# Per-node update steps on GpSimd behind a mask, and count reads placed by the steps beside them, in a two-layer graph kernel

## Chip, cores and metric

The kernel runs on one core of a Trainium2 chip. The metric is the time of the device in microseconds, the median of several runs. The engines are TensorE (PE, with its weight loads PEld), VectorE (DVE, `V` in the code), ScalarE (ACT, `A`), GpSimd (POOL, `G`) and SyncE (SP).

## The reference

There are 3327 nodes with 64 features each and an adjacency matrix `adj` of zeros and ones. The kernel pads 3327 to 26 blocks of 128. Cut to what matters:

```python
# layer 0: hyperbolic attention between connected nodes
h = relu(layernorm(x))
adj_att = sigmoid(left[:, None] + right[None, :] + b) * adj     # left, right from logmap0(h) @ w_att
support = einsum('ij,ijd->id', adj_att, logmap(h_i, h_j, c))    # a sum over neighbours j
x = x + proj(expmap(h, support, c), c)                          # node by node
# layer 1: a weighted sum over the last 100 neighbours of a row
h = relu(layernorm(x)); support = h @ weight
rank = cumsum(adj != 0, axis=1); deg = rank[:, -1:]; k = min(deg, 100)
pos = rank - (deg - k)
w = (adj != 0) * where(pos > 0, 0.5 ** (k - pos), 0)
x = x + w @ support + bias
```

Layer 0 has a large part for each pair of nodes (i, j) and a small part for each node i. Layer 1 needs, for each pair, how many neighbours of i come after j (the "count").

## The kernel before

`fast` does the work; `general` is a fall-back that a run-time flag selects and that isn't used with these inputs. The destination nodes i are cut into four strips of 8, 8, 6 and 4 blocks (`STRIPS`), and for each strip the source blocks j are walked from 25 down to 0. A strip of 8 or 6 blocks takes one source block in a round, the last strip two, so that a round has at most 1024 columns: 26, 26, 26 and 13 rounds, n = 0 to 90, so that strip 1 begins at round 26, strip 2 at 52 and strip 3 at 78. The text calls the strips 0 to 3.

In a round the engines do this:

- DVE: `edges` (L621) writes the mask of the adjacency block, in bf16; `pair_one` (L666) multiplies the attention by the adjacency; `pair_two` (L671) multiplies the result with the pair function out of PSUM.
- ACT: `gelus` (L870, L871), two activations in place in PSUM; `sigmoids` (L661), the attention's tanh.
- PE: `count` (L632, L633) adds the mask to a running count in PSUM; `products` (L678, L679) prepares the pair function; `total` (L691) sums over j.
- One of ACT (L650) and DVE (L652, L654) carries out `read`: it copies the count of this source block out of PSUM into `behind_lo`, `behind_hi` or `weight_of`, as integers. The next `count` has to wait for it. `ON_ACT` gives, for each strip, the share of the reads that go to ACT: 1/2, 5/8, 3/4, 1/2. In the last strip a round has two reads.

When a strip has ended, its sums are turned (`strip_out`, `turn`, `per_node`), and the per-node part, `post`, runs as a generator beside the rounds of the next strip. It is cut into portions: each `yield` ends one, and its value is what the portion counts. `BIG` (4) is a wide step of DVE, over all features of the strip's nodes; `LATER` (99) ends the portions of this call; `ACT` (100) asks for an activation, which is issued later in a round by `asked_of_act`. `advance(PORTIONS[k])` takes portions worth 4 once a round in strips 1 and 2, and worth 8 twice a round in strip 3. Many small steps, on one value a node, go to GpSimd while `hidden` is true, that is for the nodes of strips 0, 1 and 2; `after(time)` then lets as many calls pass as `time` takes at the round times in `ROUND`. For the last strip's nodes the small steps run on DVE and only the powers on GpSimd.

The steps of `post` in order: a product and two reduces (L1077 to L1081); small steps; a tanh on ACT (L1101); small steps; four wide steps that update x (L1137 `w`, L1139 `u`, L1141 and L1143 the additions to `xs`); a reduce (L1146) and a centring (L1148); a square on ACT (L1151) and a reduce (L1153); small steps; the features of layer 1 (L1159, L1162 on ACT, L1164). The wide steps of a strip's nodes run in the rounds of the strip after it.

Layer 1 comes last. Its matmuls (L1328) run over the source blocks in an order that has those of strip 3 at the end; `decode` (L1311 on ACT, L1314 and L1315 on DVE) turns counts into weights, and the rest of the per-node part of strips 2 and 3 runs beside it. GpSimd adds the bias (L1333).

The order on PE, DVE and ACT is the order in which the program issues (`manual_schedule`); each engine works through its own queue, and semaphores hold an instruction until its inputs are there. The main loop issues a round as follows:

```python
        gelus(n)
        asked_of_act()
        ...
        pair_one(n)
        if two:
            read(m, js(m)[0])
        if EARLY <= m + 1 < R:
            edges(m + 1)
```

after which come `count(m)`, `sigmoids(n + 1)`, the other `read(m)`, `products(n + 1)`, `pair_two(n)` and `advance`, with m = n + 1. So behind a mask on DVE stand, at most, a read and then `pair_two`.

Of the kernel before, what the change touches and what calls it, by code (L numbers as in the profile page):

```python
# [13 lines left out]
BF16 = mybir.dt.bfloat16  # L14
# [8 lines left out]
P = 128  # L23
N = 3327
NB = 26
# [7 lines left out]
AHEAD, LOADS = 1, 4  # L33
EARLY = 3
SGB, ADB = 5, 5
ON_ACT = ((1, 2), (5, 8), (3, 4), (1, 2))


PORTIONS, LAST = (2, 4, 4, 8), 8
BIG, LATER, ACT = 4, 99, 100  # L40
ROUND = (3.5, 3.5, 2.8, 1.9)

LEAD = 4
# [404 lines left out]
def fast(ctx, tc, x, adj_t, r, w_att, b_att, weight, bias, out, flag):  # L448

    nc = tc.nc  # L450
    V, A, G, T = nc.vector, nc.scalar, nc.gpsimd, nc.tensor
# [73 lines left out]
    def wide(t, n):  # L525
        return t[:, :, None].to_broadcast([P, n, D])
# [15 lines left out]
    post_pool = ctx.enter_context(tc.tile_pool(name="post", bufs=1))  # L542
# [3 lines left out]
    def behind(j):  # L546
        if j in JD:
            return weight_of[:, j - JD.start]
        return behind_of["lo"][:, j] if j < JD.start else behind_hi[:, j - JD.stop]
# [16 lines left out]
    ad_of, mask_of, sg_of, pq_of = {}, {}, {}, {}  # L566
# [36 lines left out]
    def span(n):  # L603
        k, lo, hi = rounds[n]
        return (hi - lo) * strips[k].F

    def js(n):
        k, lo, hi = rounds[n]
        return range(hi - 1, lo - 1, -1)
# [8 lines left out]
    def edges(n):  # L618
        mask_of[n] = mask = work.tile([P, FMAX], BF16, name="mask", bufs=3)
        args = mask[:, : span(n)], ad_of[n][:, : span(n)]  # L620
        V.tensor_scalar(*args, 0.0, None, op0=ALU.not_equal)  # L621
# [14 lines left out]
    def by_parity(t):  # L636
        return t.rearrange("p (r k) -> p r k", r=2)

    def read(n, j, on_act=None):
        k, lo, hi = rounds[n]  # L640
        S = strips[k]
        kept = behind(j)[:, S.i0 : S.i0 + S.F]
        num, den = ON_ACT[k]
        i = NB - 1 - j
        of = S.pc[:, : S.F]
        if j in JD:
            kept = by_parity(weight_of[:, j - JD.start])[:, :, S.i0 // 2 : (S.i0 + S.F) // 2]
            of = of.rearrange("p (k r) -> p r k", r=2)
        if on_act or (on_act is None and i * num // den != (i + 1) * num // den):
            A.activation(kept, of, AF.Relu, scale=128.0 if j in JD else 1.0)  # L650
        elif j in JD:
            V.tensor_scalar(kept, of, 0.0, 128.0, op0=ALU.max, op1=ALU.mult)  # L652
        else:
            V.tensor_scalar(kept, S.pc[:, : S.F], 0.0, None, op0=ALU.max)  # L654

    def sigmoids(n):

        S = strips[rounds[n][0]]
        sg_of[n] = sg = work.tile([P, FMAX], F32, name="sg", bufs=SGB)
        for j in js(n):  # L660
            A.activation(part(n, sg, j), S.left[:, : S.F], AF.Tanh, bias=right[:, j : j + 1], scale=0.5)  # L661
# [48 lines left out]
    def small(name):  # L710
        return pre.tile([P, NB], F32, name=name)
# [8 lines left out]
    m, rs = (small(n) for n in ("m", "rs"))  # L720
    v2, y2, t2 = (pre.tile([P, 2, NB], F32, name=n) for n in ("v2", "y2", "t2"))
    v, y = v2[:, 0], y2[:, 0]
    for hs in node_halves:
        n = hs.stop - hs.start
# [166 lines left out]
    for j in js(0):  # L891
        read(0, j, True)
# [10 lines left out]
    for b in (24, 20, 16, 12, 8, 4, 0):  # L903
        n = min(4, NB - b)
# [59 lines left out]
    def range_steps():  # L964
        t1 = post_pool.tile([P, NB], F32, name="st1")
        V.tensor_mul(t1, nrm, node)
        V.tensor_reduce(st[:, 0:1], t1, AX.X, ALU.max)
        yield 2
        V.scalar_tensor_tensor(t1, x2, c_c, t1, op0=ALU.mult, op1=ALU.mult)
        V.tensor_reduce(st[:, 1:2], t1, AX.X, ALU.max)  # L970
        yield 2
        V.tensor_mul(t1, bal, node)
        V.tensor_reduce(st[:, 2:3], t1, AX.X, ALU.max)
        yield 2
        V.tensor_reduce(st[:, 3:4], t1, AX.X, ALU.min)
        V.tensor_scalar(st[:, 3:4], st[:, 3:4], -1.0, None, op0=ALU.mult)
# [21 lines left out]
    class Asked:  # L998


        def __init__(self, engine, to):
            self.engine, self.to = engine, to

        def __getattr__(self, name):
            return lambda *args, **kwargs: self.to.append((getattr(self.engine, name), args, kwargs))

    def post(agg, k):


# [3 lines left out]
        b0, nb = STRIPS[k]  # L1013
        bs = slice(b0, b0 + nb)
        hidden = k + 1 < len(STRIPS)
# [3 lines left out]
        def tile_of(name, *dims):  # L1019
            return pool.tile([P, *dims], F32, name=name if hidden else name + "_last")  # L1020

        def mul(y, a, b):
            W.tensor_mul(y, a, b)
# [32 lines left out]
        def after(time):  # L1056

            for do, args, kwargs in asked_of_w:
                do(*args, **kwargs)  # L1059
                if not hidden:  # L1060
                    yield from [LATER] * 2 if kwargs.get("op") == ALU.pow else [1]
            asked_of_w.clear()
            if hidden:
                yield from [LATER] * math.ceil(time / ROUND[k + 1])
# [4 lines left out]
        hs, v, xs = hw[:, bs, :D], agg[:, :, :D], x_sb[:, bs]  # L1069

        dots, of_sum, of_end = tile_of("dots", 3, nb), tile_of("of_sum", 2, nb), tile_of("of_end", 2, nb)
        d, e = tile_of("d", 2, nb), tile_of("e", 2, nb)
        t0, t1, k_, y2, rn, rt = (tile_of(n, nb) for n in ("t0", "t1", "k", "y2", "rn", "rt"))
        u, w = tile_of("u", nb, D), tile_of("w", nb, D)
# [21 lines left out]
        root(rn, t0)  # L1096
        mul(t0, t0, rn)
        mul(t0, t0, sk[:, bs])
        yield from after(8.5)
        yield ACT  # L1100
        A.activation(k_, t0, AF.Tanh)  # L1101
        yield 0
# [31 lines left out]
        mul(of_end, of_end, both(rn))  # L1134
        mul(of_end[:, 0], of_end[:, 0], ih[:, bs])
        yield from after(16)
        V.tensor_mul(w, hs, wide(of_end[:, 0], nb))  # L1137
        yield BIG
        V.tensor_mul(u, v, wide(of_end[:, 1], nb))  # L1139
        yield BIG  # L1140
        V.tensor_add(xs, xs, w)  # L1141
        yield BIG
        V.tensor_add(xs, xs, u)  # L1143
        yield BIG

        V.tensor_reduce(t0, xs, AX.X, ALU.add)  # L1146
        yield BIG
# [50 lines left out]

    class Stage:
        def __init__(self, portions):  # L1200
            self.portions, self.asked = portions, False

    def advance(portions):
        for stage in stages:
            while portions > 0 and not stage.asked:
                portion = next(stage.portions, LATER)
                stage.asked = portion == ACT
                if portion >= LATER:
                    break
                portions -= portion  # L1210

    def asked_of_act():
        for stage in stages:
            if stage.asked:
                next(stage.portions)
                stage.asked = False

    def finish():
        for stage in stages:
# [4 lines left out]
    stages, rest_of_ahead = [Stage(range_steps())], last_of_ahead()  # L1224
# [3 lines left out]
    for n in range(2, R):  # L1228
        k, lo, hi = rounds[n]
        m, w = n + AHEAD, span(n)  # L1230
        ended, turned = (n > i and rounds[n - i - 1][1] == 0 for i in (1, 2))
        if n + LOADS < R:
            if rounds[n + LOADS][2] == NB:
                strip_in(rounds[n + LOADS][0])
            load(n + LOADS)
        fresh = EARLY <= m < R
        two = fresh and len(js(m)) == 2
        if two:
            count(m, js(m)[0])
        apart = k + 1 == len(STRIPS)  # L1240
        if turned and not apart:
            pa = turn(k - 1)
        if n >= 4 and (apart or not turned):
            total(n - 2)
        gelus(n)
        asked_of_act()
        if turned and not apart:
            finish()
            stages.append(Stage(per_node(k - 1, pa)))
        pair_one(n)  # L1250
        if two:
            read(m, js(m)[0])
        if EARLY <= m + 1 < R:
            edges(m + 1)
        if n == 2:
            for j in js(2):
                read(2, j, True)
        if n < 4:
            products(n + 1)
        if fresh:  # L1260
            count(m, js(m)[-1])
        if n + 1 < R:
            sigmoids(n + 1)
        if fresh:
            read(m, js(m)[-1])
        if 4 <= n < R - 1:
            products(n + 1)
        if n == 2:
            total(1)
        if ended:  # L1270
            strip_out(k - 1)
        if hi - lo > 1:
            advance(PORTIONS[k])
        if turned and apart:
            pa = turn(k - 1)
        pair_two(n)
        if turned and apart:
            finish()
            stages.append(Stage(per_node(k - 1, pa)))
        if n < 4:  # L1280
            next(rest_of_ahead)
            continue
        advance(PORTIONS[k])
        if turned and not apart:
            total(n - 2)
        if n > R - 3:
            next(range_end)
# [11 lines left out]
    with tc.tile_pool(name="l1", bufs=2, reuse_waits="tile") as l1, tc.manual_schedule(engines=IN_ORDER):  # L1299
# [35 lines left out]
        for i, j in enumerate(order):  # L1335
            for jn in every[: i + 1 + LEAD]:
                if jn not in weights:
                    weights[jn] = decode(jn)
            asked_of_act()
            advance(LAST)  # L1340
            for n in range(len(chunks)):
                add(j, weights[j], n)
            if i % 4 == 3 and i < STRIPS[-2][0]:
                bias(i - 3, 4)
# [93 lines left out]
```

## Time and profile before

| | us |
|---|---|
| median of 3 runs | 404.73 (404.49 to 406.21) |
| the profiled execution, whole | 406.06 |
| its span | 404.3 |
| busy in the span: PE, DVE, ACT, POOL | 353.7, 366.7, 355.8, 117.7 |

The span is what the profile covers, from the first to the last instruction. The profiled execution was 1.3 us longer than the median of the runs, so a change that is worked out from its rows is taken off its own time and then carried over to the median. On the timeline a row gives the start, the duration, the engine, the line, the operation, output and inputs, and shapes. Durations of one engine overlap by about 0.1 us, so that what an instruction costs its engine is better read from one start to the next. Round n is found by its L870 on ACT: round 31 starts at 145.45, round 32 at 149.35, round 40 at 178.07, round 50 at 214.15, round 54 at 227.97, round 57 at 237.26, round 76 at 292.65, round 90 at 346.71. The matmuls of layer 1 begin at 354.11.

### The profile page before, as it was taken

The page shows a single profiled execution, that of the slowest core. Times are in us where ns is not written, and L with a number is a line of the kernel's source. Part 1 is how long each engine was busy: PE and PEld are TensorE (multiplying, and loading weights), DVE is VectorE, ACT ScalarE, POOL GpSimd, SP SyncE. Part 2 cuts the span into 40 slices and gives each one's busy share as a digit, 9 for nine tenths or more (in the row PEclk, how much of TensorE's full clock was granted, in tenths as well). Part 3 has the DMA queues.
Part 4 walks back from the last instruction along what each step waited for, and adds up shares of the span by engine and source line. Part 5 has one row for each costly group of instructions (what it writes and reads, how often), then busy time and mean ns, then how long its engine had stood idle before and what let it go on. Part 6 is the DMA issues. An engine that isn't in the chain of part 4 may idle for free.

```text
span 404.3 us, 4738 instructions
## 1 busy us (share of the span) xinstructions
PE 353.7 (87%) x1460; PEld 150.3 (37%) x1460; DVE 366.7 (91%) x563; ACT 355.8 (88%) x407; POOL 117.7 (29%) x240
## 2 busy tenths in 40 slices
PE   0077899999999899999999899999979899899992
PEld 0053333333333333333333444444433333254462
DVE  3999899999999989999999999899999999899831
ACT  3589999999999899999999999999998999858710
POOL 8145200000000053870052052850240767241200
PEclk9999999999999899999999999999999999999997
DMA  7314545454547434543434435444563340000012
GB/s 208 142 42 133 170 144 154 131 159 148 160 146 229 152 107 156 156 155 107 153 115 149 149 119 156 133 139 120 158 191 106 114 148 0 0 2 1 2 39 54
DMA packets 23298, 48.99 MB, mean 121 GB/s; under 512 B 8789, under 2 KB 9245, under 8 KB 23265
## 3 DMA queue, kind: packets, MB, share of 16 engines
q1 hardware_dynamic: 20993, 47.66, 38.1%
q10 hardware_dynamic: 1808, 0.46, 0.6%
q0 software_dynamic: 464, 0.49, 0.5%
q8 instruction: 13, 0.21, 0.2%
q14 instruction: 20, 0.16, 0.1%
HBM read 46.40 MB, written 0.87 MB: 117 GB/s over the span
## 4 chain that ended last, share of the span: by engine, by line
DVE 39%; PE 24%; ACT 23%; issue 10%; DMA 1%; DVEq 0%; ACTq 0%
DVE sg L671 13%; DVE sg L666 11%; PE pw L1328 9%; ACT pq L870 7%; ACT sg L661 7%; PE po L691 6%; DVE behind_lo L654 3%; ACT pq L871 3%; ACT behind_lo L650 2%; PE pq L678 2%; PE pq L679 2%; DVE behind_hi L654 2%; DVE mask L621 2%; PE pc L632 2%; PE pw L1370 2%
## 5 line engine op out<-in xcount | busy, mean ns | idle before, releaser
L691 PE MATMUL po<-sg,hw 128*65 128x512 f32 (+1 forms) x364 | 160.2, 563 | 0.4 <-DVE st L987 0.4
L671 DVE SCALAR_TENSOR_TENSOR sg<-pq,sg 128x1024 f32<-128x1024 f32 (+1 forms) x91 | 103.7, 1140 | 4.3 <-ACT pq L871 3.8
L666 DVE SCALAR_TENSOR_TENSOR sg<-sg,ad 128x1024 f32<-128x1024 f32 (+1 forms) x91 | 104.2, 1146 | 0.2
L661 ACT ACTIVATE sg<-left_b,right 128x1024 f32<-128x1024 f32 (+2 forms) x103 | 99.5, 978 | 0.0
L871 ACT ACTIVATE pq<-pq 128x1024 f32<-128x1024 f32 (+1 forms) x91 | 86.2, 947 | 2.9
L870 ACT ACTIVATE pq<-pq 128x1024 f32<-128x1024 f32 (+1 forms) x91 | 87.1, 957 | 1.6 <-PE pq L679 1.3
L691 PEld LDWEIGHTS po<-sg,hw 128*65 128x65 f32 x364 | 49.2, 138 | 68.9 <-issue 54.2
L632 PE MATMUL pc<-mask,ca 128*128 128x512 bf16 (+1 forms) x175 | 63.5, 363 | 11.0 <-ACT behind_hi L650 3.2
L678 PE MATMUL pq<-iu,ju 71*128 71x512 f16 (+1 forms) x182 | 67.0, 368 | 1.7 <-ACT jz L807 0.8
L633 PE MATMUL pc<-mask,cb 128*128 128x512 bf16 (+1 forms) x182 | 64.9, 367 | 2.7 <-ACT behind_lo L650 1.7
L679 PE MATMUL pq<-iz,jz 128*128 128x512 f16 (+1 forms) x182 | 65.5, 367 | 0.0
L621 DVE TENSOR_SCALAR mask<-ad 128x1024 bf16<-128x1024 f32 (+1 forms) x91 | 58.8, 647 | 0.0
L1059 POOL TENSOR_TENSOR dots<-dots,ih 128x8 f32<-128x8 f32 (+1 forms) x3 | 3.7, 1223 | 131.0 <-DVE dots L1079 131.0
L633 PEld LDWEIGHTS <-cb 128*128 128x128 bf16 x182 | 17.7, 97 | 52.2 <-issue 40.5
L1328 PE MATMUL pw<-wt,s 128*128 128x512 bf16 (+1 forms) x154 | 31.4, 364 | 0.0
L632 PEld LDWEIGHTS <-ca 128*128 128x128 bf16 x175 | 17.1, 98 | 30.3 <-issue 18.0
L678 PEld LDWEIGHTS <-ju 71*128 71x128 f16 x182 | 17.9, 98 | 23.6 <-DVE sg L671 5.9
L679 PEld LDWEIGHTS <-jz 128*128 128x128 f16 x182 | 18.0, 99 | 18.9 <-issue 2.0
L650 ACT ACTIVATE behind_lo<-pc 128x1024 uint8<-128x1024 f32 (+2 forms) x29 | 24.9, 859 | 0.0
L1328 PEld LDWEIGHTS <-s 128*128 128x128 f16 x182 | 17.8, 99 | 18.2
L1333 POOL TENSOR_TENSOR x_sb<-x_sb,bias_b 128x256 f32<-128x256 f32 (+1 forms) x6 | 8.3, 1394 | 51.9 <-DVE w L1148 46.0
L650 ACT ACTIVATE behind_hi<-pc 128x1024 uint8<-128x1024 f32 (+2 forms) x25 | 21.8, 871 | 1.6 <-PE pc L633 1.5
(318 smaller groups left out, 347.3 us busy)
## 6 DMA issues: line engine op xcount, KB each, us to landing
ad<-in_adj_t SPq DMA_DIRECT2D x65, 512.0 KB, 3.5
ad<-in_adj_t SPq DMA_DIRECT2D x26, 384.0 KB, 3.1
out<-o SPq DMA_DIRECT2D x6, 128.0 KB, 1.9
left_b<-left_d SPq DMA_DIRECT2D x1, 512.0 KB, 4.3
x_sb<-in_x ACTq DMA_DIRECT2D x1, 416.0 KB, 5.5
x_sb<-in_x SPq DMA_DIRECT2D x1, 416.0 KB
left_b<-left_d SPq DMA_DIRECT2D x1, 384.0 KB
jz<-iz POOLq DMA_DIRECT2D x2, 128.0 KB, 2.6
```

What stands on the lines that cost most here:

```text
L621: V.tensor_scalar(*args, 0.0, None, op0=ALU.not_equal)
L632: T.matmul(S.pc[:, f0:f1], ca, S.before[:, f0:f1], start=False, stop=True, skip_group_check=True)
L633: T.matmul(S.pc[:, f0:f1], cb, now[:, f0:f1], start=S.first, stop=True, skip_group_check=True)
L661: A.activation(part(n, sg, j), S.left[:, : S.F], AF.Tanh, bias=right[:, j : j + 1], scale=0.5)
L666: V.scalar_tensor_tensor(sg, sg, 1.0, ad_of.pop(n)[:, :w], op0=ALU.add, op1=ALU.mult)
L671: V.scalar_tensor_tensor(sg, pq_of.pop(n)[:, :w], WD, sg, op0=ALU.add, op1=ALU.mult)
L678: T.matmul(part(n, pq, j, f0, f1), ju[:KB, j, :], S.iu[:, f0:f1], start=True, stop=False)
L679: T.matmul(part(n, pq, j, f0, f1), jz[:, j, :], S.iz[:, f0:f1], start=False, stop=True)
L691: T.matmul(po[: D + 1, : f1 - f0], hw[:, j, :], part(n, sg_of[n], j, f0, f1), start=j == NB - 1, stop=j == 0)
L870: A.activation(pq, pq, AF.Gelu, scale=-WG / QS)
L871: A.activation(pq, pq, AF.Gelu, scale=WH)
L1328: T.matmul(pw[n], s2[:, j].rearrange("p c d -> p (c d)"), w if r is None else w[:, r], start=j == order[0], stop=j == NB - 1)
```

## The change

The four wide update steps go from DVE to GpSimd for the nodes of strips 0, 1 and 2. Each is asked for with `yield POOL` and issued by a new `asked_of_pool`, straight after a mask was issued on DVE. Ahead of it GpSimd copies one column of that mask into `seen`, so that in GpSimd's queue the step comes after a wait for the mask. One step goes out in a round. Where no mask is issued in a round any more, or in layer 1, the step is issued without the copy. After the fourth step one call passes (`LATER`) before DVE goes on. The last strip's nodes keep their wide steps on DVE.

`ON_ACT` goes. In a strip with one read a round, a read goes to ACT if a portion that counted `BIG` was taken since the last read (`wide_step`); the other reads go to ACT and DVE in turn. In the last strip the lower of the two blocks is read on ACT and the other on DVE. The time that is let pass ahead of the tanh goes from 8.5 to 7.

```diff
-ON_ACT = ((1, 2), (5, 8), (3, 4), (1, 2))
-BIG, LATER, ACT = 4, 99, 100
+BIG, LATER, ACT, POOL = 4, 99, 100, 101
...
-        num, den = ON_ACT[k]
-        i = NB - 1 - j
+        if hi - lo > 1:
+            on_act = j == lo
...
-        if on_act or (on_act is None and i * num // den != (i + 1) * num // den):
+        if on_act is None:
+            on_act = wide_step[0] or not last_on_act[0]
+            if not wide_step[0]:
+                last_on_act[0] = on_act
+            wide_step[0] = False
+        if on_act:
             A.activation(kept, of, AF.Relu, scale=128.0 if j in JD else 1.0)
...
+    def tensor_mul(engine, *args):
+        engine.tensor_mul(*args)
+
+    def tensor_add(engine, *args):
+        engine.tensor_add(*args)
+
+    seen = post_pool.tile([P, 1], BF16, name="seen")
...
-        yield from after(8.5)
+        yield from after(7)
         yield ACT
...
         yield from after(16)
-        V.tensor_mul(w, hs, wide(of_end[:, 0], nb))
-        yield BIG
-        V.tensor_mul(u, v, wide(of_end[:, 1], nb))
-        yield BIG
-        V.tensor_add(xs, xs, w)
-        yield BIG
-        V.tensor_add(xs, xs, u)
-        yield BIG
+        for op, *args in ((tensor_mul, w, hs, wide(of_end[:, 0], nb)), (tensor_mul, u, v, wide(of_end[:, 1], nb)),
+                          (tensor_add, xs, xs, w), (tensor_add, xs, xs, u)):
+            if hidden:
+                yield POOL
+                op(G, *args)
+                yield 0
+            else:
+                op(V, *args)
+                yield BIG
+        if hidden:
+            yield LATER
...
                 portion = next(stage.portions, LATER)
-                stage.asked = portion == ACT
+                wide_step[0] |= portion == BIG
+                stage.asked = portion if portion in (ACT, POOL) else None
...
-    def asked_of_act():
+    def asked_of(engine):
         for stage in stages:
-            if stage.asked:
+            if stage.asked == engine:
                 next(stage.portions)
-                stage.asked = False
+                stage.asked = None
+
+    def asked_of_pool(n):
+        if any(stage.asked == POOL for stage in stages):
+            G.tensor_copy(seen, mask_of[n][:, :1])
+            asked_of(POOL)
...
         if EARLY <= m + 1 < R:
             edges(m + 1)
+            asked_of_pool(m + 1)
+        elif n > 4:
+            asked_of(POOL)
...
-            asked_of_act()
+            asked_of(ACT)
+            asked_of(POOL)
             advance(LAST)
```

More of the change, by code (lines that the diff above doesn't have):

```diff
@@ L654, in read @@
             V.tensor_scalar(kept, S.pc[:, : S.F], 0.0, None, op0=ALU.max)
+    wide_step, last_on_act = [False], [False]
     def sigmoids(n):
@@ L1200, in __init__ @@
         def __init__(self, portions):
-            self.portions, self.asked = portions, False
+            self.portions, self.asked = portions, None
     def advance(portions):
@@ L1338, in fast @@
                     weights[jn] = decode(jn)
-            asked_of_act()
+            asked_of(ACT)
+            asked_of(POOL)
             advance(LAST)
```

## The prediction

> **What bounds the kernel now.** I read the busy table first, the chain of waits second, then windows over the strips, then the timeline of three engines in a few rounds. The page alone doesn't decide:
>
> ```profile
> PE 353.7 (87%) x1460; PEld 150.3 (37%) x1460; DVE 366.7 (91%) x563; ACT 355.8 (88%) x407; POOL 117.7 (29%) x240
> DVE 39%; PE 24%; ACT 23%; issue 10%; DMA 1%; DVEq 0%; ACTq 0%
> ```
>
> The first line has DVE busiest, the second (the chain, by engine) has DVE in front. Both suggest that work taken off DVE pays in full. The windows say otherwise. The first row runs from ScalarE's start on round 32 to its start on round 54 (the bulk of strip 1 and the entry to strip 2), the second from round 57 to round 76 (strip 2). Columns: busy time of PE, weight loads, DVE, ACT, POOL.
>
> ```profile
> 149.35:227.97 78.62, 75.55 (x265) 28.58 (x263) 77.28 (x86) 77.92 (x86) 30.27 (x56) 1.00 0.46 144
> 237.26:292.65 55.39, 52.03 (x231) 24.89 (x230) 51.78 (x70) 54.79 (x74) 22.91 (x53) 1.00 0.48 142
> ```
>
> ACT is busy for 77.92 of 78.62 us and for 54.79 of 55.39: it has no idle time there. DVE has 1.3 and 3.6 us free. So in strips 1 and 2, where the edits lie, **ScalarE's own work sets the time, with DVE close behind**. The timeline of ScalarE in strip 1 gives its price list:
>
> ```profile
> 188.01 1.01 ACT L650 ACTIVATE behind_lo<-pc 128x1024 uint8<-128x1024 f32 x1
> 188.92 1.02 ACT L870 ACTIVATE pq<-pq 128x1024 f32<-128x1024 f32 x1
> 189.97 1.01 ACT L871 ACTIVATE pq<-pq 128x1024 f32<-128x1024 f32 x1
> 190.90 1.14 ACT L661 ACTIVATE sg<-left_b,right 128x1024 f32<-128x1024 f32 x1
> 191.94 1.01 ACT L870 ACTIVATE pq<-pq 128x1024 f32<-128x1024 f32 x1
> ```
>
> From start to start, two gelus and a tanh (L870, L871, L661) take 191.94 - 188.92 = 3.02 us a round, and a count read (L650) adds 0.91. The same timeline in strip 2 (768 wide) gives 2.37 and 0.70. DVE in strip 1, start to start: 1.14 (L666) + 0.60 (mask, L621) + 1.13 (L671) = 2.87 a round, 1.13 for a read (L654), 0.60 for a wide step. In strip 2: 2.20, 0.86, 0.60. PE: eight bf16 or f16 matmuls at 0.216 plus the 1.72 us sum of L691 = 3.45 a round in strip 1, three quarters of it (2.59) in strip 2.
>
> [...]
>
> ```profile
> 201.52 1.22 DVE L666 SCALAR_TENSOR_TENSOR sg<-sg,ad 128x1024 f32<-128x1024 f32 x1
> 202.65 0.69 DVE L621 TENSOR_SCALAR mask<-ad 128x1024 bf16<-128x1024 f32 x1
> 203.25 1.22 DVE L654 TENSOR_SCALAR behind_lo<-pc 128x1024 uint8<-128x1024 f32 x1
> 204.39 1.21 DVE L671 SCALAR_TENSOR_TENSOR sg<-pq,sg 128x1024 f32<-128x1024 f32 x1
> 201.68 2.92 POOL L1333 TENSOR_TENSOR x_sb<-x_sb,bias_b 128x256 f32<-128x256 f32 x2 [21.23 <-DVE w L1148]
> ```
>
> Two GpSimd additions of 256 elements take 2.92 us here; the shortest single one of L1333 in this trace takes 0.717. [...] In the other direction I see holds too: L666 at 30.44 takes 1.40 us and L919 at 33.02 takes 0.99 while L905 runs on GpSimd; elsewhere they take 1.22 and 0.68 to 0.69. [...] from the trace's shortest 256-element product (L905, 0.604) it is at most 1.21. I take 1.2, and 0.9 for 384.
>
> **The change, part by part.**
>
> *Wide steps to GpSimd.* Twelve DVE instructions go: eight of 0.60 and four of 0.47 (start to start), 6.7 us. In their place come twelve GpSimd products and sums at 1.2 or 0.9, and eight copies `seen` of one column, about 0.2 each (small copies of L1059 take 0.19). The four steps of strip 2's nodes find no later mask, so they have no `seen`; they run one behind the other after the small chain, which ends at 342.2 now, and are over by about 347. A released step starts about 0.3 us after the mask. [...] A 1.2 us step ends at 1.5. It delays the next L666 by 0.4 us where ScalarE reads, by nothing where DVE reads; in strip 2 by 0.6 or 0. The reads alternate in those four rounds, so the cost on DVE is 2 x 0.4 = 0.8 in strip 1 and 2 x 0.6 = 1.2 in strip 2. Bounds: 0, and a whole step (1.2) each. Behind the waiting `seen` on GpSimd's queue stands only its step; behind that, the reduce of L1146 on DVE, and a whole further round is put between them. A mask buffer is now also held by `seen`, but three buffers rotate.
>
> *Reads.* I followed the rule by hand. Strip 1: 6 reads are marked by a wide step and go to ScalarE, the other 20 alternate (10 there): 16, as before. Strip 2: 8 marked, 9 of 18 alternating: 17 instead of 19, and DVE reads 9 instead of 7. Strip 3: the lower block of a round reads on ScalarE, which is what 1/2 gave. Strip 0: alternating, as before.
>
> *ScalarE's sum.* Strip 2: two reads fewer, -1.4 us. Strip 1: equal count, moved. Rounds 25 to 30 have one read more, where ScalarE waits for PE (its starts there are 5.57 us apart); only about 0.5 of its 0.91 stays. Rounds 31 to 39 have 5 instead of 6: -0.9. Rounds 40 to 49 have 6 and 6. Net -0.4.
>
> *DVE's cover.* Rounds 40 to 49 cost DVE 28.7 + 4 reads 4.5 + 7 small steps 4.2 = 37.4 now, against ScalarE's 36.1; DVE falls 2.2 us behind and ScalarE doesn't stop, so the buffers carry that much. Afterwards: 37.4 - 2.4 + 0.8 = 35.8, under 36.1. In strip 2, rounds 68 to 75: 17.6 + 3 x 0.86 + 1.8 + 1.2 = 23.2 against ScalarE's 8 x 2.37 + 5 x 0.70 + 0.42 = 22.9, inside what the buffers carry. So the removed 4.8 us buy almost nothing by themselves: they only keep DVE from being late at the turn into strip 3 (rounds 77 to 82, where DVE sets the pace): -0.2.
>
> *Strip 3 and the end.* ScalarE sets 3.77 us a round there, unchanged. At the end L1137 to L1148 lie ahead of the last L671 on DVE; without them the last sums on PE may start up to 0.6 us earlier (PE's queue is full until then). GpSimd's steps collide with DVE there, so I take -0.3.
>
> *Layer 1.* The reduce and centring of strip 2's nodes move into it: +0.9 us of DVE. Last strip's features are written at 382.2 and PE first wants them near 385.2 (the first bank is read out at 386.07, four matmuls later), so 3 us cover it. Asking for the tanh earlier (7 for 8.5) costs nothing: in strips 1 and 2 it comes a round sooner, and GpSimd idles 6.4 and 8.3 us for it now; in strip 3 the round stays the same.
>
> Sum: -0.4 - 1.4 - 0.2 - 0.3 = **-2.3 us**. The profiled execution took 406.06 (span 404.3), so it would be 403.8; against the median of 404.73, 402.4.
>
> **Rivals.** (a) The sum above: 402.4, chance 0.50. (b) *DVE is the bound, as the chain has it.* Then 6.7 us less, two reads more (1.7): -5.0, 399.7. For it: 91% and 39%. Against: ScalarE's missing idle time. Chance 0.07. (c) *Nothing to be told from before*: ScalarE's 1.8 us are there, but GpSimd's holds give half back at the DVE-paced turn; 403.9, chance 0.28. This holds the case that the moved reads just trade idle time. (d) [...] a step begun after the mask runs into L666 and holds it in every one of the eight rounds of strips 1 and 2. DVE's slack is 1.1 us of strip 1 after the removal and a little under that in strip 2; with the 2.3 gained, 8 holds must exceed 4.3 us, 0.54 each, before the kernel is slower. Held for the whole 1.2 each: 9.6 - 4.3 = +5.3, 410.0; at 0.8 each, +2.1. [...] Chance 0.15.
>
> **Numbers.** About 0.5% (2.0 us) is what a measurement of this kernel can tell from no change. (a) lies 0.3 us beyond that line, and its terms are uncertain by 1.2 us in all, so some of it falls inside. Faster 0.52, same 0.34, slower 0.14. Range 400.4 to 406.0: down to near (b), up through (c) to the mild end of (d).
>
> **What would show it.** Right: ScalarE still without idle time in rounds 32 to 76, with 17 reads in strip 2; GpSimd's steps of 1.2 to 1.5 us that start after a mask; L666 late by about 0.4 us in every second of these rounds; layer 1 as long as before. Wrong: ScalarE waiting for `pq` or `sg` in rounds 40 to 45 or 68 to 72 [...], steps of over 2 us, or a longer gap ahead of the last strip's matmuls.

## The result, and the profile after

The changed kernel takes 405.36 us (median of 22 runs) where the kernel before took 405.87 beside it (22 runs): ratio 0.9998, interval 0.9987 to 1.001. Nothing that this measurement could tell apart has changed; the 0.5 us between the medians lies at the edge of that interval. The forecast was 402.4, 2.3 us faster than a median of 404.73. That median was of three runs; of 22 it is 405.87, so 1.1 us of the 3.0 between forecast and result come from the start of the sum and not from its terms.

In the page after, DVE is as busy as before, although twelve wide steps left it, and it still leads the chain of waits:

```profile
PE 354.5 (88%) x1460; PEld 151.0 (37%) x1460; DVE 367.1 (91%) x553; ACT 354.6 (88%) x405; POOL 135.7 (34%) x260
DVE 38%; ACT 28%; PE 18%; issue 12%; DMA 1%; DVEq 0%; ACTq 0%
```

DVE has ten instructions fewer (twelve steps went, two reads came) and is busy 0.4 us *longer* (366.7 before). So others of its instructions became longer. The windows of rounds 32 to 54 and 57 to 76 (same cuts as before, columns as before) place it: DVE is busy 2.9 us more in the second (54.72 for 51.78). There the four steps that left took 2.7 us; three reads more (eight instead of five) take 2.9, and the same 19 masks and 19 L672 take 2.3 more.

```profile
149.35:227.97 78.62, 75.17 (x266) 28.83 (x265) 77.27 (x83) 77.72 (x85) 34.57 (x60) 1.00 0.48 141
237.26:292.65 55.39, 53.46 (x237) 25.36 (x236) 54.72 (x70) 54.30 (x73) 31.37 (x58) 1.00 0.50 140
```

The timeline of GpSimd and of DVE in strip 1 of the changed kernel says why. L1014 and L1017 are the wide steps, L1238 is the copy into `seen`, L658 the count read on DVE, L672 is `pair_one`, L620 the mask:

```profile
177.24 1.04 POOL L1014 TENSOR_TENSOR u<-agg,of_end 128x512 f32<-128x512 f32 x1
178.24 2.02 POOL L1014 TENSOR_TENSOR w<-hw,of_end 128x512 f32<-128x512 f32 x1
180.34 1.59 POOL L1017 TENSOR_TENSOR x_sb<-x_sb,w 128x512 f32<-128x512 f32 x1
182.01 1.27 POOL L1017 TENSOR_TENSOR x_sb<-x_sb,u 128x512 f32<-128x512 f32 x1
183.23 1.19 POOL L1238 COPY seen<-mask 128x1 bf16<-128x1 bf16 x1
185.11 0.19 POOL L1238 COPY seen<-mask 128x1 bf16<-128x1 bf16 x1 [0.69 <-DVE mask L620]
```

```profile
177.56 1.80 DVE L672 SCALAR_TENSOR_TENSOR sg<-sg,ad 128x1024 f32<-128x1024 f32 x1
179.29 1.53 DVE L620 TENSOR_SCALAR mask<-ad 128x1024 bf16<-128x1024 f32 x1
180.74 1.21 DVE L658 TENSOR_SCALAR behind_lo<-pc 128x1024 uint8<-128x1024 f32 x1
```

**The gate is not there.** All four steps run in a row as soon as the small steps end, `u` even ahead of `w`, and the copies come after them. `IN_ORDER` holds PE, DVE and ACT, not GpSimd; its instructions were put in another order than the program's, and no step depends on `seen`. The unguarded steps hold DVE: L672 takes 1.80 instead of 1.21, the mask 1.53 instead of 0.68. Summed over the instructions after 140 us, such holds are 1.6 us in strip 1, 2.4 in strip 2 and 0.4 in strip 3.

**An account by stretches.** I cut the traces at ScalarE's starts of the first gelu of a round, at the start of layer 1's first matmul and at the end of its last. Two executions of the kernel before agree to 0.02 us in every stretch, so small differences can be read. The first column is the length before, the others are differences to it, in us:

```
rounds    before  changed  no_seen  no_wide  late_order  turn_reads  at_once  all_three
0-29      109.33   -0.02     0.00    +0.19     +0.49       +0.17      -0.04    +0.05
29-30       5.57   +0.01    -1.64    -1.64     -1.64       -1.64      -1.64    -0.09
30-40      36.03   -0.41    -0.40    -0.38     -0.40       -0.96      -0.40    -0.88
40-51      39.99   +0.37    +0.30    -0.01     -0.03       +1.78      +0.32    +0.03
51-55      13.76    0.00    -0.01    +0.01      0.00        0.00       0.00    +0.02
55-56       2.39   +1.36    +1.34    +1.34     +1.36        0.00      +1.35     0.00
56-68      34.79   -1.41    -1.41    -1.39     -1.42       -1.41      -1.42    -1.37
68-76      23.65   -0.02    -0.02    -0.70     -0.71        0.00      +0.01    -0.67
76-83      27.82   -0.29    -0.30    -0.30     -0.30       -0.29      -0.30    -0.29
83-90      26.24   -0.06    -0.06    -0.06     -0.06       -0.06      -0.06    -0.04
90-layer1   7.40   -0.61    -0.62    -0.61     -0.61       -0.60      -0.23    -0.24
layer 1    43.11   +0.65    +0.66    +0.81     +0.62       +0.64       0.00     0.00
sum       370.08   -0.43    -2.16    -2.74     -2.70       -2.37      -2.41    -3.48
```

(no_seen and the others are the experiments below; `at_once` is `strip3_at_once`.) The changed kernel gains 2.8 us in five stretches (30 to 40, 56 to 68, and the three from 76 to layer 1) and gives 2.4 back in three: rounds 40 to 51, 55 to 56 and layer 1. Rounds 68 to 76 should have gained 0.7 and didn't.

Two of the stretches go with TensorE's granted clock. In each of the fourteen profiles of this case 29 to 30 takes 5.5 to 5.6 us where a stretch of half clock begins in round 28, and 3.9 where none does; 55 to 56 takes 3.7 us in the ten profiles with one that begins in round 54, and 2.4 in the four without (the kernel before, twice, `turn_reads` and `all_three`). The windows 134.4 to 137.8 in the kernel before, and both places in the changed one and in `turn_reads` (the clock is the third number from the end):

```profile
134.40:137.80 3.40, 3.40 (x8) 1.15 (x7) 3.40 (x5) 3.37 (x5) 0.00 (x0) 0.58 0.46 140
```

```profile
134.40:137.80 3.40, 3.40 (x9) 1.21 (x7) 3.40 (x5) 3.37 (x5) 0.00 (x0) 0.64 0.51 140
230.00:233.40 3.40, 3.40 (x8) 1.19 (x7) 2.43 (x5) 3.37 (x6) 0.00 (x0) 0.64 0.46 130
```

```profile
134.40:137.80 3.40, 3.40 (x11) 1.17 (x9) 3.40 (x5) 3.37 (x5) 0.00 (x0) 1.00 0.47 137
230.00:233.40 3.40, 3.40 (x15) 1.57 (x14) 2.68 (x5) 3.37 (x6) 0.00 (x0) 1.00 0.51 163
```

Both places are turns from one strip to the next, where PE waits for the sums to be copied (1.83 us at the first in the changed kernel, 0.84 and 0.62 at the second). The changed kernel's two stretches of half clock are 3.41 us long (133.47 to 136.88 and 229.04 to 232.45, a granted clock of 0.50 in both). In the 3.41 us ahead of them PE was busy for 1.57 and 1.96 us, at a clock of 1.00. As much idle time isn't always followed by one: at the turn into strip 3 of the kernel before PE was busy for 1.67 of 3.41 us (294.00 to 297.41), and the clock is 1.00 there and in the 3.41 us after it. What sets off a stretch isn't shown. ScalarE's extra read of round 55 stands at the same turn, so that the 1.36 us there can't be put down to the read alone.

### The profile page after: what moved, and what is told of

Read it like the earlier page. It is cut to its first block, busy times and chain, and to the rows that moved or that the text cites. A ratio compares the mean times of both kernels' runs of the same rounds, so it can differ in the third digit from the quotient of the medians.

```text
span 404.6 us, 4764 instructions
## 1 busy us (share of the span) xinstructions
PE 354.5 (88%) x1460; PEld 151.0 (37%) x1460; DVE 367.1 (91%) x553; ACT 354.6 (88%) x405; POOL 135.7 (34%) x260
## 4 chain that ended last, share of the span: by engine, by line
DVE 38%; ACT 28%; PE 18%; issue 12%; DMA 1%; DVEq 0%; ACTq 0%
DVE sg L677 10%; DVE sg L672 9%; ACT sg L667 8%; ACT pq L876 8%; PE po L697 7%; ACT pq L877 4%; DVE behind_lo L658 3%; ACT behind_lo L654 2%; PE pq L684 2%; ACT behind_hi L654 2%; PE pq L685 2%; PE pc L631 2%; PE pc L632 2%; DVE mask L620 2%; PE pw L1397 2%
## 5 line engine op out<-in xcount | busy, mean ns | idle before, releaser
L677 DVE SCALAR_TENSOR_TENSOR sg<-pq,sg 128x1024 f32<-128x1024 f32 (+1 forms) x91 | 103.7, 1140 | 5.2 <-ACT pq L877 4.7
L672 DVE SCALAR_TENSOR_TENSOR sg<-sg,ad 128x1024 f32<-128x1024 f32 (+1 forms) x91 | 106.9, 1175 | 0.2
L620 DVE TENSOR_SCALAR mask<-ad 128x1024 bf16<-128x1024 f32 (+1 forms) x91 | 60.5, 666 | 0.0
L654 ACT ACTIVATE behind_lo<-pc 128x1024 uint8<-128x1024 f32 (+2 forms) x28 | 24.1, 860 | 0.0
L654 ACT ACTIVATE behind_hi<-pc 128x1024 uint8<-128x1024 f32 (+2 forms) x25 | 21.8, 871 | 2.2 <-PE pc L632 2.1
L658 DVE TENSOR_SCALAR behind_lo<-pc 128x1024 uint8<-128x1024 f32 (+2 forms) x20 | 20.1, 1003 | 0.1
```

What stands on the lines that cost most here:

```text
L672: V.scalar_tensor_tensor(sg, sg, 1.0, ad_of.pop(n)[:, :w], op0=ALU.add, op1=ALU.mult)
L677: V.scalar_tensor_tensor(sg, pq_of.pop(n)[:, :w], WD, sg, op0=ALU.add, op1=ALU.mult)
```

## The experiments

Theory A: ScalarE's work sets the pace, and what it gained was lost where the unguarded steps hold DVE, at the turn and in layer 1. Theory B: DVE had room for the holds. Rival: DVE sets the pace.

**The copies removed** (`no_seen`).

```diff
...
-            G.tensor_copy(seen, mask_of[n][:, :1])
```

> The changed kernel without the copies of the mask into seen; nothing else. Theory A: the copies gate nothing, so GpSimd's steps stay where they are and the starts of the rounds agree with those of the changed kernel to 0.1 us. If the copies did hold something back (a mask buffer, or the steps), rounds 40 to 46 or 68 to 74 would move by 0.3 us or more.

Ratio to before 0.9981 (0.9963 to 1.0). Apart from 29 to 30 the stretches agree with the changed kernel's within 0.07 us, and the holds on DVE are the same to 0.02 us (0.59, 0.85, 0.17 in strip 1). The copies gate nothing.

**The wide steps left out, and put back on DVE.** In `wide_on_dve` `op(G, *args)` is `op(V, *args)`; in `no_wide` the line is gone. Neither has `seen`.

> The changed kernel with the twelve wide steps of strips 0 to 2 left out, on GpSimd and DVE both (x of these nodes is not updated by layer 0). It is the most that taking these steps off DVE can bring. Theory A: no holds, so ScalarE's 0.4 and 0.7 us come back: 0.8 to 1.3 us ahead of the changed kernel, and not more, since ScalarE's own work is unchanged. Theory B: within 0.2 us of it. Rival (DVE sets the pace): 4 us ahead.

> The changed kernel with the twelve wide steps back on DVE, at the place where GpSimd's were asked for (behind a mask, one a round); reads and tanh as in the changed kernel. Theory A (ScalarE sets the pace, DVE close behind): DVE has 6.7 us more of its own and 4.4 us of holds less, so it stands about 2.3 us worse over three strips, most of it covered: 0 to 1 us after the changed kernel. Rival (DVE sets the pace, as the chain says): 2 us or more after it.

`no_wide`: ratio 0.9952 (0.9934 to 0.997), 1.8 us below before in the medians (403.74 against 405.56). Without any wide step rounds 40 to 51 are even with the kernel before and 68 to 76 gain 0.70: against the changed kernel that is 0.38 and 0.68. So the holds cost 1.06 us there, close to the 0.4 and 0.7 expected. The median is 1.5 us under that of `no_seen`, which ran beside it (403.74 for 405.24). The rival, with 4 us, falls.

`wide_on_dve`: ratio 1.0012 (0.999 to 1.0034). Rounds 40 to 51 take 0.57 more than before, 68 to 76 take 0.40 less, layer 1 takes 1.59 more since two of its wide steps moved into it. The median is 0.7 us over that of `no_seen` (405.90 for 405.24), within what was expected. Set against `no_wide`, which differs from it in the twelve steps alone, it is 2.2 us slower: 0.58 in rounds 40 to 51, 0.30 in 68 to 76, 0.27 in 76 to 83, 0.79 in layer 1 and 0.37 in the opening (rounds 0 to 29). So 6.7 us of DVE are worth about 2 us here: DVE is not the bound, but it isn't free either. In strip 2, work on DVE is cheaper than the unguarded steps on GpSimd (-0.40 against -0.02), in strip 1 dearer (+0.57 against +0.37).

**GpSimd kept in order** (`gpsimd_in_order`, whole main part; `late_order`, from round 20).

```diff
...
+        if n == 20:
+            ordered.close()
+            ordered.enter_context(tc.manual_schedule(engines=IN_ORDER | {mybir.EngineType.Pool}))
```

> The changed kernel with GpSimd's queue, too, kept in the order in which the main loop issues, so that each wide step really stands behind its copy of the mask. Theory A (the gate is missing in the changed kernel: the four steps ran in a row before any of the copies and held DVE's L672 and mask for 4.4 us): the steps start 0.2 to 0.4 us after a mask, DVE's stretched instructions add up to at most 2 us, ScalarE gets about 0.4 us back in strip 1 and 0.7 in strip 2, and the kernel ends 0.5 to 1 us before the changed one, near 404.3 where that has 405.0. Theory B (DVE had room for the holds, what was lost was lost on ScalarE at the turns): the steps move, the time does not (within 0.2 us).

> As the kernel with GpSimd's queue kept in order, but only from round 20 on, so that the opening of the kernel, which had become 4.1 us longer there, stays as in the changed kernel. Theory A: the opening is back to the changed kernel's; the wide steps stand behind their masks, ScalarE's loss of 0.37 us over rounds 40 to 51 and 0.68 us over rounds 68 to 76 are gone, and the kernel ends about 1 us ahead of the changed one, less if a stretch of half clock falls badly. Theory B: no difference (within 0.2 us).

The first is 0.59% slower (1.0059, 1.004 to 1.0079): GpSimd's products and loads of the opening were put in order too, and rounds 0 to 29 take 4.1 us more. It was expected ahead of the changed kernel and isn't; in rounds 40 to 51 and 68 to 76 it does what was expected (0.00 and -0.69). `late_order` keeps that and loses the opening's cost: ratio 0.9978 (0.9959 to 0.9997). Its GpSimd in strip 1:

```profile
178.24 0.19 POOL L1239 COPY seen<-mask 128x1 bf16<-128x1 bf16 x1 [2.16 <-DVE mask L620]
178.38 1.04 POOL L1015 TENSOR_TENSOR w<-hw,of_end 128x512 f32<-128x512 f32 x1
182.30 0.19 POOL L1239 COPY seen<-mask 128x1 bf16<-128x1 bf16 x1 [2.89 <-DVE mask L620]
182.44 1.04 POOL L1015 TENSOR_TENSOR u<-agg,of_end 128x512 f32<-128x512 f32 x1
185.30 0.19 POOL L1239 COPY seen<-mask 128x1 bf16<-128x1 bf16 x1 [1.82 <-DVE mask L620]
185.43 1.28 POOL L1018 TENSOR_TENSOR x_sb<-x_sb,w 128x512 f32<-128x512 f32 x1
```

and its DVE around the second step:

```profile
181.49 0.68 DVE L620 TENSOR_SCALAR mask<-ad 128x1024 bf16<-128x1024 f32 x1
182.09 1.21 DVE L677 SCALAR_TENSOR_TENSOR sg<-pq,sg 128x1024 f32<-128x1024 f32 x1
183.23 1.33 DVE L672 SCALAR_TENSOR_TENSOR sg<-sg,ad 128x1024 f32<-128x1024 f32 x1
```

A product takes 1.04 us, starts 0.3 us after the mask's end and overlaps L672 by 0.25; L672 is held for 0.12. Where DVE reads a count in between, it isn't held at all. The holds fall to 0.47 us in strip 1 and 1.02 in strip 2, and ScalarE doesn't feel them (-0.03 and -0.71, as without any wide step). Theory B falls, by these stretches: they are the same in `gpsimd_in_order`, `late_order` and `no_wide`. The medians alone would not show it, since the interval of `late_order` overlaps that of the changed kernel.

**The reads at the turns** (`turn_reads`).

```diff
+        if n in (31, 56):
+            on_act = False
```

> The changed kernel with two count reads given back to DVE: those issued in rounds 30 and 55, at the turns into strips 1 and 2, where the rule marks three reads in a row for ScalarE. Theory A (part of the loss is the reads that ScalarE takes at the turns): ScalarE's start of round 31 comes about 0.5 us earlier and that of round 56 by 0.7 to 1.4 us, kept up to round 76; DVE has 1.5 us or more to spare there. The kernel ends 1 us ahead of the changed one or a little more. If DVE has no room at the turns, the gain is gone by round 40 and round 60.

Ratio 0.9999 (0.9983 to 1.0016): the expected gain is not there. In the trace its parts came, 0.55 us more in rounds 30 to 40 and 1.36 in 55 to 56, but rounds 40 to 51 cost 1.78 instead of 0.37. The 1.36 is not the read's alone, for in this trace the clock is whole at that turn (1.00 at 230 to 233.4, above): two things changed at once. ScalarE arrives earlier, and the unguarded steps now meet other instructions of DVE. Two masks in a row are held, 1.53 and 1.76 for 0.68; the counts behind them come late, and ScalarE waits for PE at 182.38:

```profile
ACT behind_lo L656 <- PE pc L632: 0.8, 1, 0.8
ACT pq L878 <- PE pq L687: 0.4, 1, 0.4
```

So four unguarded steps cost 0.4 us of strip 1 in one trace and 1.8 in the other, depending on where they fall; in `gpsimd_alone` below they cost nothing.

**Strip 2's steps issued at once** (`strip3_at_once`).

```diff
             if hidden:
-                yield POOL
+                if k < 2:
+                    yield POOL
                 op(G, *args)
-                yield 0
+                if k < 2:
+                    yield 0
...
-            yield LATER
+            yield from [LATER] * (1 if k < 2 else 2)
```

> The changed kernel with the four wide steps of strip 2's nodes issued to GpSimd together in strip 3, so that the reduce and the centring behind them fall in strip 3, as before the change, and not in layer 1. Theory A (layer 1 became 0.65 us longer because these two DVE steps and what waits for them moved into it, and an ScalarE decode came 0.5 us late): from the first matmul of layer 1 to the last 43.1 us instead of 43.8; the start of layer 1 up to 0.4 us later, since two steps of 0.47 stand ahead of the last sums again. Net 0.2 to 0.7 us ahead of the changed kernel. Rival: layer 1 stays 43.8, so something else made it longer.

Ratio 0.9993 (0.9968 to 1.0017): the interval is too wide to show a gain of 0.3 us. In the trace layer 1 is back to 43.11 us and its start gives 0.38 back: net 0.27 ahead, as expected. So the two moved DVE steps and what waits behind them did lengthen layer 1. In the changed kernel PE waited for an ACT decode:

```profile
PE pw L1354 <- ACT wt L1337: 0.5, 1, 0.5
```

**The two halves alone.** `gpsimd_alone` has the reads of `ON_ACT`; `reads_alone` is the kernel before with the changed kernel's reads.

> The kernel before with the reads of strips 1 and 2 shared out as in the changed kernel; wide steps on DVE at their old places. Theory A: rounds 30 to 40 -0.4, rounds 55 to 56 +0.7 (+1.4 with a stretch of half clock there), rounds 56 to 68 -1.4; rounds 40 to 51 and 68 to 76 depend on DVE, which keeps four wide steps in each (0 to +1.5 and 0 to +1). Layer 1 as before. Net -1 to +1 us. If it is 1 us or more ahead of the kernel before, the reads were worth having alone and the move to GpSimd is what spoils them.

> The changed kernel with the reads shared out as before the change (ON_ACT); the wide steps on GpSimd, the copies and the earlier tanh stay. Theory A (ScalarE sets the pace, so what leaves DVE buys nothing, and the ungated steps hold DVE): rounds 30 to 40, 55 to 56 and 56 to 68 as before the change, rounds 40 to 51 and 68 to 76 within 0.5 us of it on either side, layer 1 0.65 us longer, the last rounds up to layer 1 0.6 shorter: within 0.5 us of the kernel before. Rival (DVE sets the pace): 2 us or more ahead of it.

> The kernel with the reads shared out as before and the wide steps on GpSimd, once more, with more runs. Its first five timed runs had a median of 408.85 us, 3.3 above the kernel before, while its profile (a run of 406.87) agrees with that of the kernel before within 0.1 us outside the half-clock stretches. If the five runs were an accident, the median is now within 1 us of the kernel before (405.5). If it is again 2 us or more above it, most executions differ from the profiled one, and the phase in which the ungated steps fall, which the turn reads' run showed to be worth 0.3 to 1.8 us a strip, is the first suspect: the new profile would then show ScalarE 1 us or more later by round 51 or round 76.

`reads_alone`: ratio 0.9993 (0.9975 to 1.001). Its stretches: 0 to 29 +0.72, 30 to 40 -0.36, 40 to 51 +0.51, 55 to 56 +1.33 (with half clock there), 56 to 68 -1.36, 68 to 76 -0.24. In the timed runs the reads alone win as much as they lose.

`gpsimd_alone`: 1.0082 (1.0047 to 1.0117) in five runs, 1.0054 (1.0037 to 1.0072) in eighteen (a nineteenth took 964 us and is left out). The move to GpSimd alone is slower, by 1.6 us in the second medians, against my expectation of at most half a microsecond either way. The suspect that I named, the phase of the steps, doesn't show: in both profiled executions rounds 40 to 51 and 68 to 76 are within 0.02 us of the kernel before. What they do have is 1.3 us more in 55 to 56, and the second has 1.6 us more in 76 to 83 than the first, each time beside a stretch of half clock; and the end of its executions (last section) is longer by 1 us.

The timed runs point the same way. A stretch of 3.41 us at half clock loses 1.7 us of clock, 0.0042 of an execution. The mean granted clock of the eighteen runs has a median of 0.983, that of the 24 runs of the kernel before beside them 0.990: between one and two such stretches more. Where they fall in those runs, and why, isn't known, so this stays partly open.

The turn in `gpsimd_alone` also answers what the extra read costs there. Its reads are those of the kernel before, so ScalarE has no extra one in round 55; it waits for PE instead. The first line is the changed kernel's, the second that of `gpsimd_alone`:

```profile
234.60 0.81 ACT L654 ACTIVATE behind_hi<-pc 128x768 uint8<-128x768 f32 x1 [0.56 <-PE pc L632]
233.94 0.80 ACT L875 ACTIVATE pq<-pq 128x768 f32<-128x768 f32 x1 [1.20 <-PE pq L684]
```

With the read the stretch costs 1.36 us, without it 1.30. Under the half clock ScalarE waits for PE there, 0.56 us with the read and 1.20 without: the read fills a wait. No profile has the extra read with a whole clock at this turn, so its cost by itself (0.70, the duration that was forecast) is not shown.

**The kernel before, profiled again.**

> The kernel before, unchanged, profiled a second time. In the profiles so far TensorE's granted clock is 0.5 for stretches of 3.4 us: in the kernel before once, in rounds 28 and 29; in the changed kernel there and again in rounds 54 and 55, where each costs up to 1.6 us of one profile. If these stretches change from one execution to the next, this profile has them elsewhere and its round 30 starts about 1.6 us earlier against its own start. If they belong to the kernel, it repeats the first profile to 0.1 us.

In this profile the stretch of half clock came back at the same place, and the stretches of the table to 0.02 us. But it doesn't belong to every execution. At the end of the kernel, when PE is done, the clock is half for 4.2 and 4.7 us in the two profiles. That alone leaves a mean of 0.994 to 0.995, and one stretch more leaves 0.990 to 0.991, the mean of these two. Of the 170 timed runs of the kernel before that stand beside the experiments, 36 have 0.993 or more, so no such stretch, and others go down to 0.981. The two profiles of `gpsimd_alone` differ as well: the second has a stretch at 295.8 us where the first has none.

**Together** (`all_three`).

> The changed kernel with three edits together: GpSimd's queue kept in order from round 20 on, the two turn reads on DVE, and the four steps of strip 2's nodes issued at once. Theory A, from the single runs, against the kernel before, without stretches of half clock: rounds 30 to 40 -1.0, rounds 40 to 51 0 (the 1.8 us that the turn reads lost there came from a run of ungated steps that held a mask, which the order takes away), rounds 55 to 56 0, rounds 56 to 68 -1.4, rounds 68 to 76 -0.7, the rest -0.6, layer 1 0: about 3.5 us ahead, 402 us where the kernel before has 405.7. If the turn reads cost DVE in rounds 40 to 51 for another reason, 1 to 2 us of it are missing there.

Ratio 0.994 (0.9921 to 0.996): 403.49 us against 405.54, faster than the kernel before; the changed kernel's interval (0.9987 to 1.001) lies wholly above this one. Expected were 402 us and 3.5 us ahead; the medians are 2.1 us apart. In the trace it is 3.48 us shorter, in the parts that were summed beforehand, but 1.36 of its lead over the changed kernel is the turn at 55 to 56, where its clock was whole; and ten of its eighteen timed runs have a lower mean clock (0.981 to 0.983) than the profiled one (0.985). With the steps behind their masks, rounds 30 to 40 keep what the turn read wins (40 to 51: +0.03), so the 1.8 us of `turn_reads` came from the unguarded steps.

## Why the prediction was wrong, point by point

- **What bounds the kernel: right.** ScalarE's work sets the pace, and it still has little idle time (busy 77.72 of 78.62 and 54.30 of 55.39 us); leaving out steps that take 6.7 us of DVE bought about 2 us (`no_wide` against `wide_on_dve`), where rival (b) would have had nearly all of it.
- **"A released step starts about 0.3 us after the mask": this step failed.** I took the order of the program for the order of GpSimd's queue, though `IN_ORDER` names three engines and GpSimd isn't one; the description of the change says the same and is wrong there. That the change doesn't do what it says was a rival that I should have listed. The price of a step, an estimate from twice the 0.604 us of a 256-element product, was good (1.04 for a product and 1.27 for a sum, against 1.2). The delays of 0.4 and 0.6 us were an estimate too: 1.5 us less the 1.13 of L671 in strip 1 and the 0.86 in strip 2; behind a read and L671, 2.26 and 1.73 us, nothing is left. They took it that a step disturbs DVE's L666 and mask but not its L654 and L671, for which the trace before had one place: of the two additions at 201.68 the first took 2.24 us beside L666 and the mask and ended 0.58 us after the mask, the second took 0.72 beside L654 and the start of L671. In `late_order`, where the step holds, the 0.8 and 1.2 us of holds were 0.47 and 1.02, and covered. Unguarded, they were 1.6 and 2.4, not covered: +0.37 us in rounds 40 to 51 where I had 0, and in rounds 68 to 76 the read saved (0.70) was eaten. Rival (d) had such holds; its reckoning, that the kernel gets slower only if they pass 4.3 us in strips 1 and 2, fits the 4.0 that they came to.
- **ScalarE's sum, strip 1: right.** -0.4, with about 0.5 left of the extra read at round 30: -0.41 in rounds 30 to 40.
- **ScalarE's sum, strip 2: the term of PE's clock was missing.** -1.4 was made of three reads less and one more. Rounds 56 to 68 gave -1.41 as they should. The turn at rounds 55 to 56 cost 1.36 instead of the 0.70 of a read, because PE's clock was halved at 229 to 232.5; with the old reads it costs 1.30 there under half clock (`gpsimd_alone`). I had taken the 5.57 us at round 29 for a wait that belongs to the turn, when it was half clock already, and put the clock at nothing in the sum. It bears on the timed runs as well: the mean clock of the changed kernel's 22 runs has a median of 0.985, that of the kernel before 0.989 or 0.990 in each of its four sets, about one stretch less. Why the changed kernel meets more of them stays open.
- **DVE at the turn into strip 3:** -0.2 forecast, -0.29 measured. **The end of strip 3:** -0.3 forecast, -0.61 measured.
- **"3 us cover it" in layer 1: failed.** The features of the last strip did come in time, 382.99 against a need at about 384.5, but behind the same DVE steps ScalarE's decode was late. I priced one cover and there were two. +0.65 us.
- Sum: -0.43 us in the trace up to the last matmul, in place of -2.3: 1.06 from the missing gate, 0.66 from the clock at the turn and 0.65 from layer 1 went missing, and the turn into strip 3 and the end of strip 3 gave 0.4 to 0.5 more than I had. The execution times can't confirm even that, with an interval from 0.5 us faster to 0.4 slower, and some is lost outside these stretches (last section). The outcome is that of rival (c), but not by its mechanism: the turn into strip 3, where (c) had the loss, gained. The earlier tanh (7 for 8.5) was not tried alone.

## What to carry to other kernels

A dummy copy gates another instruction only if the queue's order is kept or the instruction depends on it (all four steps ran ahead of the copies in the changed kernel; in `late_order` the first starts 0.14 us after its copy); look at the built queue, or at the first profile, before pricing what a gate saves. Where two engines are both within 2% of full, count the work of the one without idle time, stretch by stretch: what leaves the other buys only what it held up (here about 2 us for 6.7). A cover has to be checked for every consumer behind the moved step, not for the one that comes last.

## What the runs showed of the hardware

- While a 512-element step of GpSimd was running, DVE's mask, 0.68 us alone, took 1.53 in the changed kernel and 1.76 in `turn_reads` and `gpsimd_alone`, and L672, 1.21 alone, took 1.80. A product, 1.04 us in `late_order`, took 2.02 in the changed kernel beside L672 and the mask. After a mask, with DVE reading PSUM (`late_order`), the product took 1.04 us and the read and L677 1.21 each, as they take in the changed kernel where GpSimd runs nothing beside them (187.76 to 191.76).
- A stretch of half clock at a turn costs 1.3 to 1.6 us of the profile (5.57 against 3.93 us for round 29, 3.74 against 2.38 for round 55). Two profiles of one kernel can agree in these stretches (the kernel before) or differ in them (`gpsimd_alone`). A difference of two single profiles has to be cut into stretches, and the clock read in each, before it is believed.
- An execution's time less the moment on its timeline at which DVE's last instruction ends is 8.5 to 9.0 us in the four profiles with the wide steps on DVE and 9.5 to 10.2 in the nine with them on GpSimd (one without any: 9.1). A part of it lies outside the span altogether: over all timed runs the execution is longer than its span by 1.7 us in the kernels without wide steps on GpSimd, by 2.0 in those with them and by 1.9 in the two of these that issue strip 2's steps at once (medians). Nothing in the traces shows why.
